# Third layer: the first unit of the second pass is prepared inside the first pass

## The chip, the cores and the metric

The kernel runs on one core of a Trainium2 chip. The metric is the device time of one execution in microseconds (us). Before the change three runs gave 3998.32, 4000.18 and 4005.41, so the median is 4000.18 us. One more execution was taken with the hardware profiler; every instruction time below is from it.

The engines go by these names: PE is TensorE, DVE is VectorE, ACT is ScalarE, POOL is GpSimd, SP is SyncE, which here only issues transfers (DMAs). Each engine works through its own queue in order and waits at the front of it. The queues run beside one another.

## The reference

The network has four layers over eight images of 56 x 56 positions and 192 channels. Each layer normalizes its input by groups of channels and adds its output to it. The change touches the third, a gated attention over windows of 8 x 8 positions:

```python
xw = _window_partition(x)
uvb = jax.nn.silu(xw @ W_uv + b_uv)
u, v, base = (uvb[..., :e], uvb[..., e:2 * e], uvb[..., 2 * e:])
qq = _rope2((base * gq_g + gq_b).reshape(-1, Wh, Ww, S), Wh, Ww).reshape(-1, N, S)
qk = _rope2((base * gk_g + gk_b).reshape(-1, Wh, Ww, S), Wh, Ww).reshape(-1, N, S)
lq = ...   # base * lq_g + lq_b, rotated by the position in the whole image
lk = ...   # the same with lk
attn = jnp.square(jax.nn.relu(jnp.einsum('bns,bms->bnm', qq * scale, qk) + rel_bias))
quadratic = attn @ v
lin_kv = jnp.einsum('bns,bne->bse', lk, v / (N * nW))
linear = lq @ jnp.sum(lin_kv, axis=0, keepdims=True)
out = u * (quadratic + linear) @ W_proj + b_proj
```

Here e is 384 and S is 128. A rotation (`_rope2`) is, in this kernel, `a * cos + b * sin`, where `a` and `b` are the base and the base with its halves exchanged, each after its own gain and offset. Since `lin_kv` is summed over all windows of all images, nothing of `linear` can be computed before every window has been seen once: that is why the layer has two passes.

## The kernel before

`layer2` handles the eight images as four pairs.

**First pass.** 52 turns (`groups`), each for up to 256 positions of both images of a pair. In turn n, TensorE projects the normalized input to values and base (`project`, L1560), into PSUM tiles of which there are three; a full turn takes two. VectorE adds the bias (`gates`, L1570) into a tile `sm`, of which there are two, and ScalarE applies Silu (L1571) into `vb`. The values are stored to device memory (`vst`, L1580). `keys` makes the rotated keys `l1`: two products and sums on GpSimd (L1589, L1590), two products on VectorE (L1594) and a sum there (L1597). Two turns later, in turn n + 2, `turn` transposes the base on TensorE (L1606) into a PSUM tile `t`, of which there is one, ScalarE copies it out (L1610) and SP stores it (`bst`, L1611); then `sum_up` adds keys times values to the running sum `kv` (L1620). The order inside a turn is written out by hand for all engines: the first projection, `turn`, `sum_up`, the jobs due in this turn, the other projections with their gates, the key tables, `keys`. `jobs` is a list of (turn, function) for work that is to be done beside the pass: weights, tables, bias rows, norms. The key tables (`key_tables`, L1530 to L1534) are prepared in turns 0, 1, 4, 7 and 10 and use a tile `tmp` of their own. Two further turns, 52 and 53, only transpose and sum. After them VectorE scales `kv` (L1669).

**Second pass.** 28 units, one for each strip of 448 positions of a pair. `fetch2` loads a unit's base (`bt`), the base with its halves exchanged (`bs`), its input `x` and its values `vt`; the loads of unit n + 2 are issued in unit n. For unit 0 the two base loads go through GpSimd's queue (L1688, L1690), all other loads through SP's. `prepare` makes three rotations: ScalarE makes `b` and `a` (L1704, L1705), GpSimd multiplies `b` by the sine table (L1715), VectorE multiplies `a` by the cosine table and adds (L1718, L1719). Then it normalizes the input (`normalize`, L1446). `attention` makes the window products (L1730), adds the bias (L1737) and squares (L1740). In unit n these are made for unit n + 1: ScalarE's part of the first two rotations stands in its queue ahead of unit n's first gate (`act`, L1793). The unit's own products (L1757, L1766, L1775, L1785) go to PSUM accumulators of which there are three, so that the second L1785 of a unit can start only when the first gate has been read out. Unit 0 has no unit before it: its loads, rotations, normalizing and attention stand between the passes. In the second pass TensorE, VectorE, ScalarE and GpSimd follow the written order, while the order of SP's transfers is left to the planner, which takes what is ready.

**Memory.** Pools of tiles are opened one after another and take memory in that order; in a pool the tiles lie in the order in which they are first asked for. When the first pass's pools are closed, the second pass's pools take the same bytes, and a tile waits for the users of whatever lay there. Before, the first pass opened `c1` (identity, key tables) ahead of `xp` (inputs), so the second pass's `bs` lay on the identity, which the last transposition reads.

## Time and profile before

| what | value |
|---|---|
| median of three runs | 4000.18 us |
| the profiled execution's own time | 4005.24 us |
| its span, first to last instruction | 4003.1 us |
| mean granted TensorE clock | 0.978 |
| first pass, first sum (L1620) to its last | 2578.4 to 2997.8 us from the start |
| second pass, first attention (L1730) to last output product (L1818) | 3012.3 to 3649.1 us |
| a full turn of the first pass | 8.57 us |
| a unit of the second pass | 22.17 us |

A row of a timeline reads: start, duration (both us), engine, line of the kernel, operation, written tile <- read tiles, partitions x elements, how many instructions were merged into the row, and in brackets how long the engine was idle before and what ended that. A row of a table of windows reads: the window, its length, the busy time of PE, PE's weight loads, DVE, ACT and POOL with the number of instructions, the granted clock as a share of full speed, the mean busy share of the 16 DMA engines and the GB/s that they moved. An engine's idle time costs nothing unless the engine that sets the end waits for it.

### The profile page before, as it was taken

To read this page: it belongs to the slowest core of one execution; us is meant where nothing else is said; L and a number is where in the kernel's file an instruction comes from. 1 tells how busy PE (TensorE), PEld (TensorE's weight loads), DVE (VectorE), ACT (ScalarE), POOL (GpSimd) and SP (SyncE) were. 2 spreads that over 40 slices of the span, in tenths; PEclk is the share of its full clock that TensorE was granted. 3 is DMA by queue.
4 is the path that set the end of the run, shared out by engine and by line. 5 is a ranking of instruction groups with operands and counts; after the bars stand their busy time and mean duration, and the time that the engine had idled before them with its cause. 6 is when DMAs were issued, how large, how long until landed. Compare 5 with 4: busy or idle time off the path is not lost. (4 is left out here: it accounts for less than half of the span.)

```text
span 4003.1 us, 115791 instructions
## 1 busy us (share of the span) xinstructions
PE 3763.2 (94%) x51036; PEld 2657.6 (66%) x51036; DVE 2400.7 (60%) x3270; ACT 1793.0 (45%) x2036; POOL 1517.7 (38%) x1325
## 2 busy tenths in 40 slices
PE   6989999999999999999799999899999999998997
PEld 4777767777776777777466666444444555556997
DVE  5646666565766666565544444576557777774664
ACT  2434444344444444443334433333335555553564
POOL 3222242222224232323433333333334545444776
PEclk9999999999999999999899999999999999999999
DMA  7856253333526343242433434556549767663333
GB/s 156 166 131 158 78 144 102 107 92 96 142 78 162 86 129 87 81 111 68 119 98 103 113 91 108 146 170 212 175 137 206 181 164 171 158 144 103 94 107 99
DMA packets 390300, 507.93 MB, mean 127 GB/s; under 512 B 176933, under 2 KB 326725, under 8 KB 388405
## 3 DMA queue, kind: packets, MB, share of 16 engines
q1 hardware_dynamic: 385621, 494.07, 48.1%
q8 instruction: 401, 6.57, 0.7%
q0 software_dynamic: 1040, 2.99, 0.3%
q10 hardware_dynamic: 3135, 3.47, 0.3%
q14 instruction: 103, 0.84, 0.1%
HBM read 344.69 MB, written 155.65 MB: 125 GB/s over the span
## 5 line engine op out<-in xcount | busy, mean ns | idle before, releaser
L384 POOL TENSOR_TENSOR qv<-s,s 128x392 f32<-128x392 f32 (+3 forms) x320 | 556.7, 1768 | 1282.1 <-ACT s L364 887.9
L356 PE MATMUL c<-x,wqv 64*128 64x392 f32 x2592 | 474.0, 511 | 12.3 <-ACT s L364 9.4
L356 PEld LDWEIGHTS c<-x,wqv 64*128 64x128 f32 x2592 | 254.2, 194 | 170.9 <-issue 13.5
L364 ACT ACTIVATE s<-c,bqv 128x784 f32<-128x784 f32 (+1 forms) x247 | 224.6, 912 | 246.8 <-PE c L356 188.0
L496 PE MATMUL c<-x,wp 64*128 64x224 f32 x2688 | 285.4, 358 | 24.5 <-DVE ot L474 13.3
L378 DVE TENSOR_TENSOR qv<-s,s 128x784 f32<-128x784 f32 (+1 forms) x160 | 242.2, 1529 | 98.4 <-ACT s L364 98.4
L416 DVE COPY ol<-c 56x1024 f32<-56x1024 f32 x184 | 221.1, 1210 | 104.2 <-PE c L411 104.2
L416 ACT COPY or<-c 56x1024 f32<-56x1024 f32 x184 | 183.6, 1007 | 220.4 <-DVE ol L416 219.4
L496 PEld LDWEIGHTS c<-x,wp 64*128 64x128 f32 x2688 | 256.9, 190 | 30.1 <-DVE ot L474 14.1
L520 DVE TENSOR_TENSOR s<-s,c 128x896 f32<-128x896 f32 x112 | 121.8, 1088 | 258.0 <-ACT s L503 237.2
L454 PEld LDWEIGHTS c<-or,ol 120*64 120x64 f32 x7168 | 217.3, 139 | 22.4 <-issue 16.0
L454 PE MATMUL c<-or,ol 120*64 120x56 f32 x7168 | 223.8, 224 | 7.3 <-DMA ol<-ed 4.1
L503 ACT ACTIVATE s<-c,bp 128x448 f32<-128x448 f32 x224 | 129.7, 630 | 205.9 <-PE c L496 203.3
L1571 ACT ACTIVATE vb<-sm 128x1024 f32<-128x1024 f32 (+1 forms) x100 | 103.9, 1040 | 263.3 <-issue 219.8
L2147 POOL TENSOR_TENSOR y<-y,s 128x448 f32<-128x448 f32 x168 | 185.0, 1101 | 87.2 <-ACT s L2126 87.2
L2116 PE MATMUL h<-ringv,am 128*64 128x57 f32 (+1 forms) x4400 | 191.0, 234 | 18.8 <-DVE ringv L2103 11.9
L1715 POOL TENSOR_TENSOR rs<-rs,sin_win 128x896 f32<-128x896 f32 x56 | 135.5, 2438 | 192.7 <-ACT rs L1704 192.7
L1560 PE MATMUL v<-wvb,wa 128*128 128x512 f32 (+1 forms) x400 | 194.4, 619 | 3.9 <-ACT wa L1446 3.5
L2116 PE MATMUL h<-ringh,am 128*64 128x57 f32 (+1 forms) x4400 | 185.5, 231 | 8.5 <-DVE ringh L2122 7.8
L1793 ACT ACTIVATE us<-c,bub 128x896 f32<-128x896 f32 x84 | 84.6, 1007 | 225.4 <-PE c L1775 142.1
L2116 PEld LDWEIGHTS h<-ringv,am 128*64 128x64 f32 x4400 | 166.6, 139 | 22.1 <-DVE ringv L2103 12.7
L1079 PE MATMUL c<-wv,xc 128*126 128x192 f32 x896 | 175.4, 339 | 0.0
(269 smaller groups left out, 7848.4 us busy)
## 6 DMA issues: line engine op xcount, KB each, us to landing
or<-tt SPq DMA_DIRECT2D x252, 196.0 KB
ol<-tt SPq DMA_DIRECT2D x252, 196.0 KB
vt<-v SPq DMA_DIRECT2D x56, 672.0 KB
v<-vb SPq DMA_DIRECT2D x96, 384.0 KB
x<-x SPq DMA_DIRECT2D x110, 168.0 KB
wqv<-in_l_w_qv SPq DMA_DIRECT2D x38, 384.0 KB
x<-in_x SPq DMA_DIRECT2D x64, 196.0 KB
x<-x SPq DMA_DIRECT2D x110, 112.0 KB
```

What stands on the lines that cost most here:

```text
L356: nc.tensor.matmul(ps[:, h, 0:n], wqv[q][rows, k, i, :], xn[rows, k, g * n : (g + 1) * n], start=(k == 0), stop=(k == 2),)
L364: nc.scalar.activation(t, ps[rows, :, 0:n], AF.Silu, bias=bqv[rows, j : j + 1])
L378: nc.vector.tensor_tensor(sub(qv[rows, 7 * g :, 64 + H - 1 :], (HH * 120, 2), (120, 7), (-1, H)), *(t.rearrange("p u (h w) -> p u h w", w= ...
L384: eng.tensor_tensor(sub(qv[rows, w0:, H - 1 - 7 * g - HH * u :], (120, w1 - w0), (-1, 7)), *(t[:, u].rearrange("p (h w) -> p w h", w=H)[:, ...
L416: copy(dst[:, :, :, i0 : i0 + 8], view[rows])
L454: nc.tensor.matmul(ps[u * 64 : (u + 1) * 64, k, v * H : (v + 1) * H], left[:, d * H : d * H + 64], right[:, d * H : (d + 1) * H], start=Tr ...
L496: nc.tensor.matmul(ps[:, h, u * n : (u + 1) * n], wps[j][rows, k, u, :], xn[rows, k, g * n : (g + 1) * n], start=(u == 0 and k == 0), stop ...
L1079: nc.tensor.matmul(out(i, u), group(i, u), wv[0], start=(u == 0), stop=True, skip_group_check=True,)
L1560: nc.tensor.matmul(out, x[:, at : at + n], wt, start=(k == 0), stop=(k == 1), skip_group_check=True,)
L1715: nc.gpsimd.tensor_tensor(view(b), view(b), tab[1], ALU.mult)
L2116: nc.tensor.matmul(ps[sides[c], y], am[a][:, m * CB : (m + 1) * CB], old[:, x], start=(n < 2), stop=True, skip_group_check=True,)
L2147: nc.gpsimd.tensor_tensor(v, v, line[:, j], ALU.add)
```

## The change

Unit 0's preparation becomes seven jobs of the first pass's last turns: in turn 46 its base is loaded (through SP), in turns 47, 48 and 49 one rotation each is made, in turn 50 its input is loaded, in turn 51 it is normalized, and in turn 52 the attention is made, in the PSUM tile `t`. The tiles for it are slots of the first pass's own pools where these are free, and a new pool `pre` for what must live on into the second pass (the third rotation, the attention, the normalized input). In the second pass these four kinds of tiles come in turns from `pre` (even units) and `wk` (odd units), one buffer in each instead of two in `wk`. `fetch2(0)` loads only the values, first, and the input, which the output needs. To make room, the key tables' `tmp` becomes a slot of `sm`, and `xp` is opened ahead of `c1`. `rotate` and `attention` now get their tiles from the caller, and the rotation's views have one dimension more.

```diff
+        pre = es.enter_context(tc.tile_pool(name="l2p", bufs=1, reuse_waits="tile"))
...
+        def rotate(r, bt, bs, i, a, b):
...
+            if i < 2:
+                view = lambda t: t.rearrange("p i (v t) -> p i v t", t=WT)
+                tab = [
+                    t.unsqueeze(1).unsqueeze(1).to_broadcast([S, 2, 7, WT]) for t in tables[0:2]
+                ]
...
+        def attention(qq, kk, pa, s, a):
...
+        def own(pool, shape, name):
+            return cx.tile(pool, shape, name, bufs=1)
...
+            xp = pool("l2x1", 2)
             c1 = pool("l2c1", 1)
-            xp = pool("l2x1", 2)
...
-                tmp = cx.tile(c1, [128, TW, S], "tmp")[:, 0:n]
+                tmp = cx.tile(wk, [128, 2, E + S], "sm").rearrange("p i e -> p (i e)")
+                tmp = tmp[:, 0 : n * S].rearrange("p (n s) -> p n s", s=S)
...
+            def lead_fetch():
+                t = cx.tile(xp, [CA, 2, 2 * SW], "xa")
+                bs, bt = lead["b"] = t[:, :, 0:SW], t[:, :, SW:]
+                cols = slice(0, SW)
+                for h in range(2):
+                    nc.sync.dma_start(bs[sides[h]], bst[0][sides[1 - h], :, cols])
+                nc.sync.dma_start(bt, bst[0][:, :, cols])
+
+            def lead_rotate(i):
+                if "r" not in lead:
+                    t = cx.tile(xp, [CA, 2, 2 * SW], "xa")
+                    lead["r"] = [t[:, :, 0:SW], t[:, :, SW:], own(pre, [S, 2, SW], "r2")]
+                bs, bt = lead["b"]
+                b = cx.tile(xp, [128, 2 * SW], "xb").rearrange("p (i t) -> p i t", i=2)
+                rotate(0, bt, bs, i, lead["r"][i], b)()
+
+            def lead_attend():
+                s = cx.tile(wk, [128, 512], "l2")[:, 0:SW].rearrange("p (v t) -> p v t", t=WT)
+                lead["at"] = own(pre, [128, 7, WT], "at")
+                attention(*lead["r"][0:2], cx.tile(psk, [128, 512], "t"), s, lead["at"])
+
+            def lead_load():
+                xa = cx.tile(xp, [CA, 2, 2 * SW], "wa")[:, :, 0:SW]
+                xb = cx.tile(xp, [128, 2 * SW], "wb")[:, 0:SW]
+                into(xa, xb, 0, 0, 1, nc.sync)
+                lead["x"] = xa, xb
+
+            last = len(groups)
+            jobs += [(last - 6, lead_fetch), (last - 2, lead_load), (last, lead_attend)]
+            jobs += [(last - 5 + k, lambda i=i: lead_rotate(i)) for k, i in enumerate((1, 0, 2))]
+            jobs += [
+                (last - 1, lambda: lead.update(xw=normalize(pre, 0, lead["x"], 1, bufs=1)))
+            ]
...
-            queue = nc.sync if n else nc.gpsimd
...
+            if n == 0:
+                vt = values()
+            else:
+                bs = cx.tile(xp, [S, 2, SW], "bs")
...
             x = load(xp, p, r, 1)
+            if n:
+                vt = values()
...
+        def side(n):
+            return wk if n % 2 else pre
...
-        todo = list(prepare(0))
-        do(todo)
-        ahead[0].append(attention(*ahead[0][2][0:2]))
+        x, _, _, vt = state.pop(0)
+        ahead[0] = [x, lead["xw"], lead["r"], vt, lead["at"]]
```

## The prediction

> **What bounds the kernel now.** I read the page's busy shares first, then the chain of work that ended last, then the timelines of single engines around the seam between the third layer's two passes, and last a table of windows over that seam.
>
> ```profile
> PE 3763.2 (94%) x51036; PEld 2657.6 (66%) x51036; DVE 2400.7 (60%) x3270; ACT 1793.0 (45%) x2036; POOL 1517.7 (38%) x1325
> ```
>
> TensorE is the bound, so only its pauses can be won. Its timeline shows one such pause at the seam:
>
> ```profile
> 2996.95 0.86 PE L1620 MATMUL kv<-vb,l 128*128 128x384 f32 x2
> 3012.30 1.76 PE L1730 MATMUL b<-r,r 128*64 128x64 f32 x28 [14.49 <-DVE r L1719]
> 3013.99 3.35 PE L1757 MATMUL c<-wa,wub 128*128 128x448 f32 x4
> 3017.14 2.20 PE L1766 MATMUL c<-r,kv 128*128 128x448 f32 x4
> 3021.64 0.99 PE L1785 MATMUL c<-at,vt 64*64 64x64 f32 x56
> 3024.17 1.67 PE L1766 MATMUL c<-r,kv 128*128 128x448 f32 x4
> ```
>
> The reader sees 14.49 us without a matmul, and then slow ones: L1757's four take 3.35 us where later ones take 1.67, the first attention 1.76 where the next (3030.50) takes 1.03. The windows say why, and what else is full:
>
> ```profile
> 2980.00:2997.00 17.00, 16.37 (x61) 7.87 (x59) 9.65 (x13) 5.97 (x8) 6.62 (x6) 1.00 0.38 130
> 2997.00:3003.00 6.00, 0.81 (x4) 0.20 (x2) 0.56 (x1) 0.70 (x2) 1.97 (x3) 0.85 0.95 267
> 3009.00:3015.00 6.00, 2.70 (x30) 2.18 (x31) 5.86 (x4) 4.21 (x6) 3.00 (x2) 0.50 1.08 233
> 3015.00:3021.00 6.00, 6.00 (x76) 3.06 (x78) 5.86 (x5) 4.91 (x5) 4.37 (x2) 0.73 1.10 234
> 3033.00:3045.00 12.00, 12.00 (x155) 6.34 (x152) 6.98 (x6) 6.71 (x7) 9.15 (x5) 1.00 0.49 97
> ```
>
> The last three columns are granted clock, DMA share and GB/s. The clock is 0.50 from about 3001 to 3018, and the DMA engines are full (0.95 to 1.10, 224 to 267 GB/s) until 3033: the seam is bound by transfers as much as by rotations. ScalarE shows who waits for them:
>
> ```profile
> 3014.91 1.13 ACT L1704 ACTIVATE rs<-bs,gbs 128x896 f32<-128x896 f32 x1 [0.71 <-DMA bs<-bs]
> 3016.30 1.13 ACT L1705 ACTIVATE r<-bt,gbs 128x896 f32<-128x896 f32 x1 [0.25 <-DMA bt<-bs]
> 3020.32 1.01 ACT L1793 ACTIVATE us<-c,bub 128x896 f32<-128x896 f32 x1 [0.84 <-PE c L1775]
> ```
>
> The first two rows already belong to unit 1; they stand in ScalarE's queue ahead of unit 0's first gate (third row), and unit 0's second product (L1785 at 3021.64) needs the accumulator that this gate frees.
>
> **What could be won at most.** An undisturbed unit without the output of a previous one takes 17.5 us (3038.50 to 3055.97 in the chain); unit 0 takes from 2997.81 to 3033.8, 36.0. With nothing late, 18.5 less 1.75 (the attention, below) = 16.8 us, 0.4%.
>
> **The rotations in turns 47 to 49.** VectorE's loop in a first-pass turn, with GpSimd's half:
>
> ```profile
> 2961.24 2.36 DVE L1570 TENSOR_TENSOR sm<-v,bvb 128x1024 f32<-128x1024 f32 x2 [1.41 <-PE v L1560]
> 2964.77 1.50 POOL L1589 TENSOR_TENSOR l<-vb,ta 128x512 f32<-128x512 f32 x1 [5.66 <-ACT vb L1571]
> 2966.35 1.33 POOL L1590 TENSOR_TENSOR l<-l,tn 128x512 f32<-128x512 f32 x1
> 2967.71 0.69 DVE L1597 TENSOR_TENSOR l<-l,l 128x512 f32<-128x512 f32 x1 [1.16 <-POOL l L1590]
> ```
>
> From gates to the end of L1597 the loop takes 7.16 us of a turn's 8.57; 1.41 is free. The change puts into it, in front of the next gates, GpSimd's product and VectorE's product and sum. These do not overlap:
>
> ```profile
> 3007.02 2.08 POOL L1715 TENSOR_TENSOR rs<-rs,sin_win 128x896 f32<-128x896 f32 x1 [1.18 <-ACT rs L1704]
> 3007.15 2.90 DVE L1719 TENSOR_TENSOR r<-r,rs 128x896 f32<-128x896 f32 x1
> 3009.97 1.08 DVE L1718 TENSOR_TENSOR r<-r,cos_win 128x896 f32<-128x896 f32 x1
> 3011.15 1.09 DVE L1719 TENSOR_TENSOR r<-r,rs 128x896 f32<-128x896 f32 x1
> ```
>
> A VectorE op beside a GpSimd one ends 0.95 after it (3009.10 to 3010.05). So the loop grows by 1.96 + 0.98 + 1.11 = 4.05 to 11.2, 2.65 over the period; after three turns the gates are 8.0 late. TensorE stands 4.41 behind the gates (2966.82, when it takes the PSUM buffer again, less 2962.41), so it loses 0.9 in turn 49 and 2.7 in turn 50. Turn 50 wins 1.4 back; turn 51 has only 5.2 us of TensorE work against a loop of 7.16, so the remaining 6.6 reach the last large sum (2994.16) whole. If the two engines overlapped, the loop would grow by 2.7 instead and about 1.6 would reach the sum. I take 6.6, because the 2.90 row is this very pair. ScalarE's two activations (1.12 each) lie in its idle 5.95 of a turn.
>
> The Trainium skill, "SBUF — State Buffer", section "Who interferes with whom", has a VectorE instruction with two SBUF inputs and a GpSimd one that reads SBUF exclude each other for a whole instruction, which speaks against this change and agrees with 2.90 against 1.09; overlap would lower the sum by 5.0.
>
> **The attention in turn 52.** 28 matmuls at 1.03, VectorE's add 0.62 and two hand-overs, because the last transpose needs the same PSUM buffer: 1.75 on the path, the square lies beside the last sum. The first pass thus ends at 2997.8 + 6.6 + 1.75 = 3006.2.
>
> **The restart.** Unit 0's values lie on the bytes of the rotated tiles, so their load (2 x 672 KB) can't be issued before the attention ends, about 3004.4. Before, the 19.0 us from 2997.3 to unit 1's last rotation input at 3016.3 carried about 4.4 MB, 232 GB/s. Now 0.92 MB (unit 0's bs and bt) is gone, and half a MB of x can go ahead; left after the last stores start at about 3002 are 0.5 MB of stores, 0.92 of unit 1's bs and bt, 1.34 of values, 0.23 of x: 3.0 MB at 240 GB/s (mean of the four rows from 2997 to 3021) is 12.5, plus 1 to land, an estimate: 3015.5, or 3017.4 with all x ahead of bt. I take 3016. Then three activations (3.2, from 3016.30 to 3019.48 before), the gate 1.05: L1785 runs at 3020.3 instead of 3021.64, 1.3 won. But TensorE has then been still from 3014.4 (stores, unit 1's bs and the values, 2.3 MB from 3002, landed at 3012.6, then 1.8 of work) and starts at half clock; the same 5.9 us at 0.50 (3012.3 to 3018.2) cost 2.9, so the seam ends 1.6 later than before. Bounds: bs and bt of unit 1 ahead of the values and no port loss: values at 3010, L1785's first run 10 earlier than its 3020.07, less 2.9: 7 won; the clock halved already in turns 50 to 52 (4.5 more, worked out below): 6.1 lost.
>
> **The table work at the start.** tmp now sits in a buffer of the gates' sums, so GpSimd's product, which ran ahead of its turn, waits for the first Silu of that turn.
>
> ```profile
> 2578.42 4.26 PE L1620 MATMUL kv<-vb,l 128*128 128x384 f32 x8 [7.22 <-DVE l L1597]
> 2575.84 1.98 POOL L1531 TENSOR_TENSOR tmp<-tb,gk 128x768 f32<-128x768 f32 x1
> ```
>
> Turn 1: this product moves to about 2579.4; L1597 before it gets shorter (2.10 to 0.69, 1.4 won), then six ops of 0.94 to 1.96 follow one another and L1597(1) ends 2.7 later, so the second sum (2588.50) starts 1.2 late. Turn 4: 2.5 later, inside the slack. Turn 7: 4.0 later, 2648.2 against a sum at 2647.05: 1.2. Turns 0 (waits for a DMA at 2567.40 anyway) and 10 (128 elements): nothing. Together 2.4; between 1.4 won and 5.
>
> **At nothing.** SP: three loads in turn 46 (1.9 us of issue) and six in turn 50 (3.0) stand ahead of stores that wait for ScalarE until 2956.15 and 2990.41, with SP idle from 2950.5 and 2983.3; uncovered, 3.0. Their 1.6 MB meet a DMA share of 0.30 to 0.44. Normalizing: 2.15 in an idle 3.92 of ScalarE in turn 51. GpSimd's three issues (1.98) go. The reshaped view: products with 14x64 and 2x448 tables took 2.06 and 2.08. Alternating pools: two buffers as before. Units 1 to 27: 22.17 us of TensorE without a pause, so what the seam gives or takes stays.
>
> **Sum.** 2.4 + 1.6 = 4.0 us slower. The profiled execution took 4005.24 (span 4003.1, 2.1 around it), 5.1 above the median of 4000.18 and inside the runs' 3998.32 to 4005.41; I add to the median: 4004.2.
>
> **The rivals.**
> - *The restart is clean (faster).* Unit 1's bs and bt get ahead of the values and the port costs little: for it, SP is not ordered by hand in the second pass, and 1.41 us a turn is free; against it, the 2.90 row. 7 won plus 1.4 at the start is 3991.8; with the clock kept up as well, up to 14 won, 3986.
> - *The clock falls inside the first pass (slower).* The pauses of 2.7 halve it from turn 50 on: the sum of 2.58, the attention, and the last transposition and sum double, 2.58 + 1.03 + 0.9 = 4.5 more, 4008.7; with 5 at the start 4011.3. For it: at 2608 to 2612 a pause of 1.66 beside small matmuls was followed by 0.51 (2612 to 2614). It decides from 4 us of such loss.
>
> **How the numbers follow.** 0.2% is 8.0 us, about what a measurement of this kernel tells from no change. My forecast, that the pause only moves, gets 0.58 and alone would span 3993 to 4008 (7 won and 1.4 at the start gone, to the point where the slower rival decides); the faster rival gets 0.17 and the slower 0.25, since a pause of 2.7 is longer than the one that was followed by 0.51. The range 3990 to 4011 takes in both rivals' prices and leaves out about 0.1 at each end: a clean restart with the clock kept up, and a halved clock with the full price at the start.
>
> **What would show it.** Right: rotation products of 2 to 3 us on VectorE in turns 47 to 49, gates late by about 2.7 more each turn, the last sum near 3006, a pause before unit 0's second L1785 with ScalarE waiting for bs or bt, clock 0.5 after it. Wrong: first-pass turns that stay at 8.57, or ScalarE's gate not held up by unit 1's loads.

## The result and the profile after

The changed kernel takes 4015.75 us (median of five runs, 4013.92 to 4023.99) where the kernel before takes 4000.18 on the same chip (five runs, 3998.32 to 4005.41). The ratio is 1.0036, interval 1.0024 to 1.0047: 14 us slower, outside the predicted 3990 to 4011. The profiled execution took 4015.75 us, its span is 4014.0.

TensorE's work is as before, from the page of the changed kernel:

```profile
PE 3769.7 (94%) x51036; PEld 2660.8 (66%) x51036; DVE 2398.4 (60%) x3270; ACT 1792.6 (45%) x2036; POOL 1516.7 (38%) x1322
```

To see where the time comes from, the third layer is cut at eight events of the two traces, and the stretches are laid side by side. All lengths are in us; a start is meant where nothing else is said. The sums are those of TensorE for turn n of the first pass (L1670 after, L1620 before), the gates are VectorE's (L1620 after, L1570 before), a unit's output product is L1854 (L1806 before), the next layer's first matmul L2176 (L2116).

| stretch | before | after | difference | predicted |
|---|---|---|---|---|
| A: end of the last matmul of the layer before, to the sum of turn 7 | 96.6 | 96.6 | 0.0 | +2.4 |
| sum of turn 7 to the gates of turn 46 | 305.6 | 305.7 | +0.1 | 0 |
| B: gates of turn 46 to gates of turn 51 | 41.3 | 47.6 | +6.2 | +6.6 |
| C: gates of turn 51 to the end of the last sum | 3.8 | 7.4 | +3.6 | +1.75 |
| D: end of the last sum to unit 0's output product | 33.6 | 31.7 | -1.9 | -6.75 |
| E: unit 0's to unit 27's output product | 610.6 | 611.9 | +1.4 | 0 |
| F: unit 27's output product to the next layer's first matmul | 17.7 | 21.8 | +4.1 | 0 |
| sum | 1109.2 | 1122.7 | +13.5 | +4.0 |

What follows F differs by 0.2 us. What comes ahead of A, where nothing was changed, was 2.5 us shorter in the trace after (2548.0 against 2550.4), so that the spans differ by 10.9 and not by 13.5; this part is 2542.7 to 2554.2 long in the traces of this document. The loss lies in B and C, as predicted but for 0.4 us less and 1.85 more, in D, where 4.9 us less was won than predicted, and in E and F, where nothing had been predicted. A, where 2.4 had been predicted, shows nothing. The letters are used below.

**B.** VectorE's timeline of the changed kernel around turn 47, and GpSimd's:

```profile
2956.80 2.55 DVE L1647 TENSOR_TENSOR l<-l,l 128x512 f32<-128x512 f32 x1 [1.17 <-POOL l L1640]
2959.27 1.08 DVE L1510 TENSOR_TENSOR xa<-xa,cos_win 128x896 f32<-128x896 f32 x1
2960.45 1.09 DVE L1511 TENSOR_TENSOR xa<-xa,xb 128x896 f32<-128x896 f32 x1
2961.47 2.35 DVE L1620 TENSOR_TENSOR sm<-v,bvb 128x1024 f32<-128x1024 f32 x2
2972.61 2.35 DVE L1620 TENSOR_TENSOR sm<-v,bvb 128x1024 f32<-128x1024 f32 x2
```

```profile
2956.72 2.08 POOL L1507 TENSOR_TENSOR xb<-xb,sin_win 128x896 f32<-128x896 f32 x1
```

The gates come 11.14 us apart (2961.47, 2972.61) instead of 8.57, where the prediction had a loop of 11.2. But it is not the rotation that meets GpSimd's product: the product starts 0.08 us ahead of the key sum L1647 of the turn before, and that sum takes 2.55 instead of 0.69. The rotation's own two operations take 1.08 and 1.09.

**C and D.** TensorE's timeline of the changed kernel at the seam, and ScalarE's:

```profile
2998.03 4.54 PE L1670 MATMUL kv<-vb,l 128*128 128x384 f32 x8 [2.59 <-DVE l L1647]
3002.50 1.04 PE L1521 MATMUL t<-xa 128*64 128x64 f32 x28
3004.27 0.33 PE L1656 MATMUL t<-ident,vb 128*128 128x128 f32 x1 [0.73 <-DVE l L1526]
3013.42 1.66 PE L1833 MATMUL c<-at,vt 64*64 64x64 f32 x51 [3.15 <-DMA vt<-v]
3025.34 1.77 PE L1833 MATMUL c<-at,vt 64*64 64x64 f32 x56 [8.66 <-ACT us L1841]
3027.04 2.86 PE L1805 MATMUL c<-wa,wub 128*128 128x448 f32 x4
```

```profile
3018.28 1.13 ACT L1494 ACTIVATE rs<-bs,gbs 128x896 f32<-128x896 f32 x1 [13.34 <-DMA bs<-bs]
3021.21 1.13 ACT L1495 ACTIVATE r<-bt,gbs 128x896 f32<-128x896 f32 x1 [1.79 <-DMA bt<-bs]
3024.30 0.98 ACT L1841 ACTIVATE us<-c,bub 128x896 f32<-128x896 f32 x1
```

The last large sum waits 2.59 us and takes 4.54 instead of 2.85: half clock. The attention (L1521) and the last transposition, which waits for its PSUM buffer, take the predicted 1.75. Then TensorE stands 8.66 us before unit 0's second product, because unit 0's first gate (L1841) stands in ScalarE's queue behind unit 1's inputs, and unit 1's bt lands at 3021.2. The table of windows shows clock, DMA share and GB/s in its last columns:

```profile
2994.00:3002.50 8.50, 5.91 (x16) 2.63 (x12) 4.04 (x7) 3.80 (x7) 3.78 (x4) 0.80 0.56 184
3005.00:3015.00 10.00, 6.06 (x77) 3.31 (x79) 0.56 (x1) 0.00 (x0) 0.00 (x0) 0.86 1.06 217
3015.00:3025.00 10.00, 1.68 (x14) 0.21 (x7) 2.52 (x2) 4.92 (x5) 3.62 (x2) 0.50 1.08 238
```

**F.** ScalarE at the start of the next layer, first before, then after; u is that layer's input tile `u0`:

```profile
3650.06 2.99 ACT L2065 ACTIVATE u<-y,co 128x3136 f32<-128x3136 f32 x1
```

```profile
3664.58 3.01 ACT L2125 ACTIVATE u<-y,co 128x3136 f32<-128x3136 f32 x1 [7.49 <-DMA x<-xb]
```

Before, ScalarE goes from unit 27's last activation straight to u. After, it and the two other engines that write u wait until unit 27's last store of x has landed.

### The profile page after: what moved, and what is told of

Its sections match the earlier page's. It is cut to its first block, busy times and chain, and to the rows that moved or that the text cites. A ratio compares the mean times of both kernels' runs of the same rounds, so it can differ in the third digit from the quotient of the medians.

```text
span 4014.0 us, 115799 instructions
## 1 busy us (share of the span) xinstructions
PE 3769.7 (94%) x51036; PEld 2660.8 (66%) x51036; DVE 2398.4 (60%) x3270; ACT 1792.6 (45%) x2036; POOL 1516.7 (38%) x1322
## 4 chain that ended last, share of the span: by engine, by line
PE 79%; DVE 8%; issue 3%; ACT 3%; DMA 3%; SPq 2%; POOL 2%; ACTq 0%; POOLq 0%; DVEq 0%
PE c L356 10%; PE h L2176 6%; PE v L1610 6%; PE c L496 5%; PE c L454 4%; PE o L529 4%; PE c L1079 4%; PE o L356 3%; PE c L1805 3%; PE y L1114 3%; PE c L1866 3%; PE c L1814 3%; PE kv L1670 2%; PE c L550 2%; PE c L1085 2%
## 5 line engine op out<-in xcount | busy, mean ns | idle before, releaser
L454 PEld LDWEIGHTS c<-or,ol 120*64 120x64 f32 x7168 | 217.3, 139 | 22.9 <-issue 17.7
L2176 PE MATMUL h<-ringv,am 128*64 128x57 f32 (+1 forms) x4400 | 191.0, 234 | 22.2 <-DVE ringv L2163 15.3
L2176 PE MATMUL h<-ringh,am 128*64 128x57 f32 (+1 forms) x4400 | 185.3, 231 | 8.7 <-DVE ringh L2182 7.8
L1841 ACT ACTIVATE us<-c,bub 128x896 f32<-128x896 f32 x84 | 84.6, 1007 | 226.1 <-PE c L1823 141.2
L2176 PEld LDWEIGHTS h<-ringv,am 128*64 128x64 f32 x4400 | 166.5, 139 | 25.5 <-DVE ringv L2163 16.2
```

The lines of the kernel that those rows point to most:

```text
L454: nc.tensor.matmul(ps[u * 64 : (u + 1) * 64, k, v * H : (v + 1) * H], left[:, d * H : d * H + 64], right[:, d * H : (d + 1) * H], start=Tr ...
L2176: nc.tensor.matmul(ps[sides[c], y], am[a][:, m * CB : (m + 1) * CB], old[:, x], start=(n < 2), stop=True, skip_group_check=True,)
```

## The experiments

All runs in one table: the ratio to the kernel before with its 95% interval, and the stretches A to F of the profiled execution. "Changed" means that an edit stands on the changed kernel, "before" that it stands on the kernel before.

| run | on | ratio | A | B | C | D | E | F |
|---|---|---|---|---|---|---|---|---|
| kernel before | | 1 | 96.6 | 41.3 | 3.8 | 33.6 | 610.6 | 17.7 |
| changed kernel | | 1.0036 (1.0024 to 1.0047) | 96.6 | 47.6 | 7.4 | 31.7 | 611.9 | 21.8 |
| e1_tmp | changed | 1.0021 (1.0008 to 1.0034) | 93.7 | 47.6 | 7.4 | 31.6 | 612.3 | 21.8 |
| e9_before_swap | before | 0.9992 (0.9982 to 1.0002) | 92.3 | 41.3 | 3.8 | 34.3 | 610.6 | 17.7 |
| e2_rest | changed | 1.0016 (1.0004 to 1.0027) | 96.6 | 43.6 | 7.3 | 31.8 | 614.3 | 21.9 |
| e10_ab | changed | 1.0017 (1.0006 to 1.0028) | 96.8 | 43.6 | 7.3 | 32.4 | 611.0 | 21.9 |
| e12_hold | changed | 1.0008 (0.9998 to 1.0018) | 96.6 | 41.4 | 5.7 | 32.2 | 611.9 | 21.8 |
| e3_order | changed | 1.0018 (1.0008 to 1.0028) | 97.0 | 47.6 | 7.4 | 26.2 | 612.1 | 21.8 |
| e8_act | changed | 1.0024 (1.0010 to 1.0039) | 96.3 | 47.6 | 5.7 | 28.2 | 613.3 | 21.8 |
| e4_layout | changed | 1.0022 (1.0011 to 1.0033) | 96.9 | 47.6 | 7.4 | 31.5 | 610.5 | 17.7 |
| e5_before_vt | before | 1.0013 (1.0002 to 1.0024) | 96.7 | 41.3 | 3.8 | 34.2 | 610.7 | 21.8 |
| e6_all | changed | 0.9984 (0.9975 to 0.9992) | 91.5 | 43.6 | 7.3 | 27.0 | 610.6 | 17.7 |
| e7_pool | changed | 0.9981 (0.9972 to 0.9991) | 94.4 | 43.6 | 5.7 | 27.1 | 612.0 | 17.8 |
| e11_best | changed | 1.0006 (0.9994 to 1.0017) | 94.1 | 43.6 | 7.4 | 29.5 | 610.9 | 17.8 |
| e13_late | changed | 1.0021 (1.0007 to 1.0034) | 93.0 | 41.4 | 5.7 | 26.0 | 627.8 | 17.8 |
| e14_hold_all | changed | 0.9974 (0.9961 to 0.9986) | 93.6 | 41.4 | 5.7 | 25.5 | 612.3 | 17.8 |
| e15_values | changed | 0.9976 (0.9965 to 0.9987) | 92.7 | 41.4 | 5.7 | 25.8 | 611.5 | 17.8 |

A ratio of 0.001 is 4 us, so the intervals alone seldom tell one edit from another; the verdicts below rest on the stretches, each of one profiled execution, which hold still where nothing was edited: B and F to 0.1, A to 0.4 (but 91.5 to 94.4 with e1's edit, of which below), D to 0.9, C to the one step of 1.7 that is told of at the end. E is not read: its intervals from unit to unit are the same 22.2, 23.7 and 24.9 us in these kernels but for the one from unit 11 to 12 (22.2 to 26.0, and unlike in kernels that do the same there; in the changed kernel TensorE waits 1.24 us in it for VectorE), and the first ones in e8 (23.5) and e13.

### The start of the first pass: e1_tmp and e9_before_swap

```diff
-                tmp = cx.tile(wk, [128, 2, E + S], "sm").rearrange("p i e -> p (i e)")
+                tmp = own(pre, [S, 2, SW], "r2").rearrange("p i e -> p (i e)")
```

> Edit: the table work's tmp no longer takes a slot of the gates' sums but the idle bytes of unit 0's third rotation (r2), so it has one buffer of its own as before. Theory (traces): the table work costs nothing, since the seventh sum ends 478.3 us after turn 1's last projection both before (2647.05 less 2568.79) and after (2644.59 less 2566.25). Then this kernel takes what the changed one took, 4015.75 within 2 us. Rival (the prediction's step): 2.4 us at the pass's start are real and were masked by something else that got faster; then the seventh sum comes about 2 us sooner after turn 1 and the time is about 4013.3.

A falls by 2.9 and the ratio to 1.0021: the rival is right (the theory's 478.3 should read 78.3). The tmp in `sm` does cost time, and something else in the change wins as much. e9 puts the order of the two pools alone into the kernel before:

```diff
+            xp = pool("l2x1", 2)
             c1 = pool("l2c1", 1)
-            xp = pool("l2x1", 2)
```

> Edit: the kernel before, with the first pass's x pool laid ahead of its constants' pool, as the changed kernel has it, and nothing else. Theory: the constants (gk and the tables) then lie on bytes that the layer before gives up earlier; this alone lets the table work start some 4 us sooner after that layer's last matmul, and the seventh sum comes 2.5 to 3 us sooner (93.7 to 94.1 instead of 96.6 after it), which is what hid the cost of tmp. Time: 2 to 3 less than before. Rival: the earlier first sum comes with the fewer loads on GpSimd's or SP's queue of the changed pass; then 96.6 as before and the time of before.

A falls by 4.4, more than expected; the time (0.8 in 1000 faster) just misses being told from no change. ScalarE in the kernel before, and then in e9:

```profile
2558.05 1.41 ACT L1446 ACTIVATE wb<-xb,norm 128x448 f32<-128x448 f32 x2 [3.51 <-DMA x<-x]
2560.15 0.34 ACTq L1627 DMA_DIRECT2D gk<-in_l_lk_gb  x1
```

```profile
2552.02 1.41 ACT L1446 ACTIVATE wa<-xa,norm 128x448 f32<-128x448 f32 x2 [7.90 <-DMA x<-x]
2555.14 0.34 ACTq L1627 DMA_DIRECT2D gk<-in_l_lk_gb  x1
```

The load of gk, the gains of the keys, is issued from ScalarE's queue behind the normalizing. Before, the last tile of that normalizing waited a second time (3.51) for a store of the layer before out of its bytes, and gk landed only at 2567.40, when GpSimd's first product of the tables could begin. With `xp` first, that second wait is gone.

Not all of 2.9 and 4.4 belongs to the edits. Between the sums of turns 3 and 4 TensorE does the small matmuls of a normalization, behind a pause. These are the windows from the one sum to the other in the kernel before, the changed kernel, e1, e9 and e6 (which does the same there as e1); the granted clock is the third figure from the end:

```profile
2605.64:2619.34 13.70, 12.04 (x45) 6.01 (x43) 11.88 (x15) 4.25 (x5) 4.57 (x3) 0.88 0.46 156
2601.18:2616.31 15.13, 13.70 (x45) 7.21 (x43) 14.67 (x15) 3.82 (x5) 8.11 (x4) 0.77 0.50 164
2594.84:2608.66 13.82, 12.04 (x44) 6.00 (x43) 12.02 (x15) 4.25 (x5) 4.70 (x3) 0.88 0.47 157
2605.14:2615.89 10.75, 10.40 (x45) 5.51 (x43) 10.49 (x14) 3.65 (x4) 3.67 (x2) 1.00 0.48 167
2596.07:2608.21 12.14, 10.40 (x44) 5.52 (x43) 11.89 (x15) 3.65 (x4) 4.67 (x3) 1.00 0.54 179
```

TensorE's busy time (10.40, 12.04 or 13.70) counts spells of 3.4 us at half clock: one in the kernel before, two in the changed kernel, one in e1, none in e9 and e6. Each costs 1.65 us, and e1 and e6 show that the same kernel code gets one or none. One such spell less is in e1's 2.9 and in e9's 4.4, so that 1.3 and 2.7 are left without it. Over all traces, A is 96.3 to 97.0 in the seven changed kernels without e1's edit (mean 96.7) and 91.5 to 94.4 in the seven with it (93.3); for the order of the pools there is the one trace.

### The last turns of the first pass: e2_rest, e10_ab and e12_hold

e2 issues VectorE's part of a rotation behind the gates of its turn:

```diff
-                rotate(0, bt, bs, i, lead["r"][i], b)()
+                lead["rest"] = rotate(0, bt, bs, i, lead["r"][i], b)
...
                         gates(g + s, pvs[s], vb, s)
+                    if "rest" in lead:
+                        lead.pop("rest")()
```

> Edit: in turns 47 to 49 VectorE's product and sum of a rotation are issued behind the turn's gates, not ahead of them; nothing else moves. Theory: the first pass ends late because the gates stand behind GpSimd's product and VectorE's two operations. Then the last sum ends 44 to 46 us after turn 47's gates (52.2 in the changed kernel, 42.6 before), the time falls by 6 to 8 to 4008 to 4010, and the large sum that took 4.54 takes 2.6 again because TensorE no longer pauses before it. Rival: GpSimd's product holds VectorE up wherever it lies (it now runs beside the gates and the key products), the turns stay above 10.5 us and the time stays within 2 us of 4015.75.

Between the two: B falls by 4.0, not by 6 to 8, the turns take 9.0 and 9.8, and the large sum still takes 4.53 after the same pause of 2.59. VectorE's key sum still meets GpSimd's product (timeline of VectorE, e2):

```profile
2959.52 2.55 DVE L1647 TENSOR_TENSOR l<-l,l 128x512 f32<-128x512 f32 x1 [1.16 <-POOL l L1640]
2969.45 2.38 DVE L1647 TENSOR_TENSOR l<-l,l 128x512 f32<-128x512 f32 x1
```

e10 adds to e2 the other order of ScalarE's two activations (`a` first), so that the product's input comes later:

```diff
-            nc.scalar.activation(b, bs, AF.Identity, bias=g[3], scale=g[1])
+            if b_first:
+                nc.scalar.activation(b, bs, AF.Identity, bias=g[3], scale=g[1])
             nc.scalar.activation(a, bt, AF.Identity, bias=g[2], scale=g[0])
+            if not b_first:
+                nc.scalar.activation(b, bs, AF.Identity, bias=g[3], scale=g[1])
...
+                lead["rest"] = rotate(0, bt, bs, i, lead["r"][i], b, False)
```

> Edit: the changed kernel with VectorE's part of a rotation behind the gates (as in the run on that), and ScalarE making a rotation's two inputs in the other order, so that the one that GpSimd multiplies comes 1.1 us later. Theory: with the product no longer ready beside VectorE's last key sum, it runs beside the gates, which read PSUM, and costs VectorE nothing: that key sum takes 0.69 instead of 2.4 in turns 46 to 48, the turns stay at 8.6, the gates of turn 51 come 41.3 to 42 us after those of turn 46 (43.6 with VectorE's part behind the gates alone, 47.6 in the changed kernel), the pause before the last large sum shrinks from 2.59 to below 1 and that sum runs at full clock. Rival: GpSimd's product holds VectorE up beside the gates just as well; then 43.6 stays.

B stays at 43.6, as the rival said, but not for its reason, as the timelines of GpSimd and VectorE in e10 show: the input still came in time, and the product got ahead by 0.07 us.

```profile
2957.37 2.07 POOL L1510 TENSOR_TENSOR xb<-xb,sin_win 128x896 f32<-128x896 f32 x1
2957.44 2.55 DVE L1650 TENSOR_TENSOR l<-l,l 128x512 f32<-128x512 f32 x1 [1.16 <-POOL l L1643]
```

So the run did not put the question. e12 does: e2 with a copy that makes GpSimd wait for the key sum.

```diff
+                held = own(pre, [128, 7, WT], "at")
+                nc.gpsimd.tensor_copy(held[:, 0], kept[max(kept)][1][:, 0, 0, 0:WT])
```

> Edit: VectorE's part of a rotation behind the gates (as before), and a small GpSimd copy ahead of GpSimd's product that reads the last key sum of VectorE, so that the product can't start before that sum has ended and runs beside the gates. (Making the two inputs in the other order had left the product ready at 2957.4, still ahead of the key sum at 2957.44.) Theory: what is left of the lateness is only the product that gets ahead of VectorE's key sum (2.4 to 2.55 instead of 0.69); now that sum takes 0.69, and the gates of turn 51 come 41.3 to 42 us after those of turn 46 (43.6 without the copy). Rival: a product beside the gates blocks VectorE all the same, the time only moves: 43 or more.

B is 41.4, that of the kernel before. GpSimd and VectorE in e12:

```profile
2973.32 0.24 POOL L1706 COPY at<-l 128x64 f32<-128x64 f32 x1 [1.14 <-DVE l L1647]
2973.58 2.09 POOL L1507 TENSOR_TENSOR xb<-xb,sin_win 128x896 f32<-128x896 f32 x1
2972.56 0.69 DVE L1647 TENSOR_TENSOR l<-l,l 128x512 f32<-128x512 f32 x1
2973.66 2.36 DVE L1620 TENSOR_TENSOR sm<-v,bvb 128x1024 f32<-128x1024 f32 x2 [0.40 <-PE v L1610]
```

The product runs beside the gates and neither is longer for it (2.09 and 2.36). The whole of B was thus two things: VectorE's 2.2 us ahead of the gates, and a product that blocked the key sum. The Trainium skill, "SBUF — State Buffer", section "Who interferes with whom", states both halves: two SBUF inputs on VectorE contend with a GpSimd operation that reads SBUF, and at most one SBUF input, outside VectorE's 2-port modes, does not. The gates have one, and 2.36 beside the product against 2.36 alone agrees; the prediction used only the first half. C falls to 5.7: the pause is 0.65, the large sum takes 2.85, and 1.9 is left, about the attention's 1.75. The ratio of 1.0008 can't be told from no change.

### The restart: e3_order, e8_act and what came of them

e3 issues unit 1's bs and bt ahead of everything of unit 0; the tiles stay where they were:

```diff
             if n == 0:
+                vt = cx.tile(xp, [128, 7, E], "vt")
+                x = cx.tile(xp, [CA, 2, SW], "xa"), cx.tile(xp, [128, SW], "xb")
+                lead["next"] = bases(0, slice(SW, 2 * SW))
+                values(vt)
+                into(*x, p, r, 1, nc.sync)
```

> Edit: SP issues unit 1's bs and bt ahead of unit 0's values and x; the tiles keep their bytes. Theory: the restart is late because of SP's order, in which bt stands behind the values and six loads of x. Then ScalarE's wait of 13.3 us for bs and TensorE's of 8.7 us for the gate are gone, unit 0's output matmul starts 24 to 27 us after the last sum (34.2 in the changed kernel, 35.9 before), and the time falls by 7 to 10, to 4006 to 4009. Rival: the transfers' total rate sets it, so the values land later by what now goes ahead of them (0.92 MB at 240 GB/s, 3.8 us), and at most 3 us are won: 4013 or more.

D is 26.2, 5.5 less, and the ratio is lower by 7 us. (The expectation counts to the output matmul L1866, which starts 34.0 us after the last sum in the changed kernel; here it is 28.6.) So the waits for bs and for the gate go as the theory had it, but its 24 to 27 us is missed by 1.6, and the rival's 3 us at most is passed. ScalarE's gate now runs at 3011.75, ahead of TensorE's need, but the values come later than they did (TensorE, e3; the last sum ends at 3003.7):

```profile
3013.18 0.47 PE L1839 MATMUL c<-at,vt 64*64 64x64 f32 x2 [5.55 <-DMA vt<-v]
3016.41 1.66 PE L1839 MATMUL c<-at,vt 64*64 64x64 f32 x51 [2.76 <-DMA vt<-v]
```

TensorE waits 8.3 us for the values where it waited 3.9, so 4.4 are given back, about the rival's 3.8: both the order and the rate count. e8 changes ScalarE's order instead:

```diff
-            rests = [next(todo, None) for _ in range(2)]
+            rests = [next(todo, None) for _ in range(2)] if n else []
...
             g0.act()
+            if n == 0:
+                rests = [next(todo, None) for _ in range(2)]
```

> Edit: the changed kernel with one thing changed: ScalarE runs unit 0's first gate ahead of unit 1's first rotation inputs; SP's order stays. Theory: TensorE's pause of 8.7 us before unit 0's second product is only ScalarE's queue (the gate behind activations that wait for bs and bt), so the pause goes, unit 0's products run at full clock, and its output matmul starts 22 to 25 us after the last sum (31.7). Rival: bs and bt are needed for unit 1's attention soon after, so that the pause only moves behind unit 0's products and the output matmul starts no earlier than 29 us after the last sum.

Nearly the rival: D is 28.2, and the interval to the next unit's output product grows by 1.3 (23.5 instead of 22.2). The pause of 8.66 is gone and comes back as one of 4.00 a few products later, in which the second gate stands behind the same inputs (TensorE and ScalarE, e8):

```profile
3025.78 3.35 PE L1805 MATMUL c<-wa,wub 128*128 128x448 f32 x4 [4.00 <-ACT us L1841]
3018.34 1.13 ACT L1494 ACTIVATE rs<-bs,gbs 128x896 f32<-128x896 f32 x1 [8.23 <-DMA bs<-bs]
```

Four kernels then tried to get below 26 with other queues. All have tmp on r2's bytes, VectorE's part behind the gates, and the tile order of e4 below; each diff shows a part of what is its own. e7: values, then bs and bt on GpSimd's queue, and e8's order on ScalarE.

```diff
+            queue = nc.sync if n else nc.gpsimd
...
-                    nc.sync.dma_start(vt[sides[i]], src)
+                    queue.dma_start(vt[sides[i]], src)
...
+                    queue.dma_start(bs[sides[h]], bst[p][sides[1 - h], :, cols])
...
+                queue.dma_start(bt, bst[p][:, :, cols])
```

> Edit: as the one with the four edits, but unit 0's values and unit 1's bs and bt (in this order) are issued by GpSimd's queue, where they don't stand behind SP's last store of bs, and ScalarE runs unit 0's first gate ahead of unit 1's rotation inputs. Theory: at the seam only the order of two queues (SP's and ScalarE's) is lost time, so unit 0's output matmul starts 18 to 21 us after the last sum (31.7 in the changed kernel, 26.2 with unit 1's bs and bt first), the clock stays at 1.0 and the time is 4 to 8 less than with the four edits. Rival: with both queues free the transfers (2.3 MB at some 240 GB/s) hold the values or bs back: 24 us or more after the last sum.

D is 27.1, the rival's: the values are issued as early as 2997.9 and land at 3007 and 3010, beside SP's x.

e11: the same with unit 0's x and unit 1's fetch on GpSimd's queue too, and e10's order. The diff's minus line is e7's.

```diff
-            queue = nc.sync if n else nc.gpsimd
+            queue = nc.sync if n > 1 else nc.gpsimd
...
+                into(*x, p, r, 1, queue)
```

> Edit: all that helped so far in the changed kernel: tmp on r2's bytes, VectorE's part behind the gates with the two inputs in the other order, x buffers ahead of the values, ScalarE's first gate ahead of unit 1's inputs, and units 0 and 1 fetched by GpSimd's queue in the order values, bs, bt, x, x, values. Theory: the seam's transfers (values 1.34 MB, then 0.92 MB) then get the DMA engines ahead of x, so unit 0's output matmul starts 21 to 24 us after the last sum (27 in the two kernels that combine), and with 2 to 4 us less in the first pass the ratio to before is 0.996 to 0.997. Rival: the transfers at the seam share the engines with x and stores in whatever order they are issued: 26 us or more, ratio 0.998.

Worse, 29.5: values and bt land earlier (3004.4 and 3007.8), but unit 1's products now stand in GpSimd's queue behind twelve loads of x and two of values, until 3014.6.

e13: GpSimd's queue with those products ahead of the x, unit 2's loads and unit 3's bs and bt on it as well, and e12's copy.

```diff
+            if n == 0:
+                do(lead["late"], 1)
             do(rests, 1)
...
             rests.append(next(todo, None))
+            if n == 0:
+                do(lead["late"])
+                state[2] = fetch2(2)
```

> Edit: all that helped (tmp on r2's bytes, VectorE's part behind the gates with the copy, x buffers ahead of the values, ScalarE's first gate ahead of unit 1's inputs), and GpSimd's queue issues unit 0's values and unit 1's bs and bt first, unit 1's two products next, and only then the x of units 0 and 1, unit 1's values and unit 2's tiles, which SP had issued at once. Theory: what the seam waits for is 2.3 MB behind other transfers; with nothing else asked for, the values land within 7 us and bt within 11 of their issue, unit 0's output matmul starts 20 to 23 us after the last sum (27.1 at best so far), and the ratio to before is 0.995 to 0.997. Rival: values, bs and bt alone fill the engines for the time that is lost, so it stays at 26 or more and the ratio at 0.998.

D is 26.0, the rival's, and the loads that were put off cost the next two units 15.5 us (33.8 and 26.1 instead of 22.2 each), so that the ratio is 1.0021.

e15: values on GpSimd's queue, bs and bt at once on SP's, e8's order, e12's copy.

```diff
+            queue = nc.sync if n else nc.gpsimd
...
-                    nc.sync.dma_start(vt[sides[i]], src)
+                    queue.dma_start(vt[sides[i]], src)
```

> Edit: as the one before, but GpSimd's queue issues unit 0's values (beside SP, which issues unit 1's bs and bt ahead of x), and ScalarE runs unit 0's first gate ahead of unit 1's inputs. Theory: values and bs, bt then start together within 3 us and share the engines only with the last stores, so that unit 0's output matmul starts 23 to 26 us after the last sum and the ratio is 0.996 to 0.997. Rival: the 2.3 MB and the rotations of unit 1 behind them fill the time in any order: 26 to 28 us, a ratio as in the kernel above.

D is 25.8, just inside the theory's range, but no less than with SP's queue alone (25.5 in e14 below), and the ratio is e14's, as the rival had it. From 2993.0 to 3004.3, when the second half of the values is there, its DMA engines are full:

```profile
2993.00:3004.30 11.30, 5.61 (x39) 2.53 (x33) 1.81 (x3) 1.27 (x2) 0.56 (x1) 0.97 0.99 214
```

So once the order is mended, D stays near 26, with TensorE still waiting 5.0 us (e15) to 8.3 us (e14) for the values: some 6 us below the changed kernel and 8 below the kernel before, and no order that was tried gets further. Values that are there before the first pass ends were not tried; their tile takes 10.5 KB in each partition.

### The start of the next layer: e4_layout and e5_before_vt

e4 asks for the x tiles ahead of the values, and issues the transfers in the changed kernel's order:

```diff
             if n == 0:
+                x = cx.tile(xp, [CA, 2, SW], "xa"), cx.tile(xp, [128, SW], "xb")
                 vt = values()
...
+                into(*x, p, r, 1, nc.sync)
```

> Edit: the second pass asks for its x buffers ahead of its values, so that the next layer's u0 lies over values, bs and bt and no longer over x; and unit 0's values no longer lie over the rotated tiles. Theory: the next layer starts 4.2 us later after the change because u0 has to wait for the last unit's stores of x out of its bytes. Then from the last output matmul of this layer to the next layer's first matmul of that line the time is back from 15.1 to about 10.9; and the values can be fetched before the attention, so that bt lands some 5 us earlier: 4015.75 less 4.2 less 3 to 5, 4006 to 4009. Rival: the later start of the next layer follows from the later end of this one (the queue of stores), not from the bytes: 15 us stay there and the time is above 4010.

(The expectation counts F from the last L1866, 6.7 us later than the table.) F is 17.7 again, exactly that of before, in a layer that ends as late as in the changed kernel. The second half of the theory failed: D is 31.5, because bs and bt stayed behind all of unit 0's x. e5 puts the fault into the kernel before:

```diff
+            vt = cx.tile(xp, [128, 7, E], "vt")
             bs = cx.tile(xp, [S, 2, SW], "bs")
...
             x = load(xp, p, r, 1)
-            vt = cx.tile(xp, [128, 7, E], "vt")
```

> Edit: the kernel before, with nothing changed but that the second pass asks for its values' buffers first, so that the last unit's x lies on bytes that the next layer's u0 takes. Theory: these bytes alone cost the next layer's start 4 us, whatever the seam does: from the last output matmul to the next layer's first matmul 21.8 us as in the changed kernel instead of 17.7, and the time about 4 us over that of before. Rival: the late start came with the changed seam; then 17.7 us and the time of before within 2 us.

F is 21.8 and the ratio 1.0013 (1.0002 to 1.0024), 5 us, with nothing else moved by more than 0.6 (D). ScalarE and TensorE in e5, then ScalarE in e4:

```profile
3651.69 3.01 ACT L2065 ACTIVATE u<-y,co 128x3136 f32<-128x3136 f32 x1 [7.44 <-DMA x<-xb]
3657.84 1.49 PE L2116 MATMUL h<-ringv,am 128*64 128x114 f32 x20 [14.64 <-DVE ringv L2103]
```

```profile
3651.74 2.99 ACT L2126 ACTIVATE u<-y,co 128x3136 f32<-128x3136 f32 x1
```

So F is the bytes and nothing else. In the kernels' memory plans u0 takes bytes 114816 to 153804 of each partition. Before, values and rotations lay there (in e4 values, bs, bt and rotations); in the changed kernel and in e5, with the values asked for first, the last x tiles lie there, among them the one of unit 27 that is stored last.

### Together: e6_all and e14_hold_all

e6 has the edits of e1, e2, e3 and e4.

> Edit: the four edits so far together in the changed kernel (tmp on r2's idle bytes; VectorE's part of a rotation behind the gates; unit 1's bs and bt ahead of unit 0's values and x; x buffers asked for ahead of the values). Theory: they touch four different places, so their gains add up: 2.9 at the pass's start, 4.0 in turns 47 to 51, 5.5 and the wait for values (some 5) at the seam, 4.1 and 1.4 behind it: 18 to 23 us less than the changed kernel, so 3993 to 3998 where that took 4015.75, a ratio to before of 0.998 to 1.000. Rival: they share a limit (transfers at the seam, the lock between VectorE and GpSimd), so that half of it comes: 4004 to 4007.

From A to F it is 19.4 us shorter than the changed kernel, within the theory's 18 to 23, and faster than the kernel before: 0.9984 (0.9975 to 0.9992), where 0.998 to 1.000 was expected. The sum is right in part by luck: D gave 4.7 where 5.5 and some 5 more were expected, and A gave 5.2 for 2.9, because two half-clock spells fell away between the sums of turns 3 and 4. e14 adds e12's copy.

> Edit: the kernel with the four edits (tmp on r2's bytes; VectorE's part behind the gates; unit 1's bs and bt ahead of unit 0's values and x; x buffers ahead of the values), plus the GpSimd copy that holds the product back. Theory: the copy wins the same 2.3 us of gates and, with the last large sum at full clock, 1.7 more; nothing else moves: some 4 us less than with the four edits, a ratio to before of 0.997 to 0.998. Rival: the seam takes it back, since its transfers don't start sooner: ratio 0.998 to 0.999 and 30 us from the last sum to unit 0's output matmul instead of 27.

0.9974 (0.9961 to 0.9986), 10 us faster than before and with e15 (0.9976) the best of all: B and C win 3.9 where 4.0 was expected, and D does not take it back (25.5). What is left of the seam is TensorE's wait for the values:

```profile
2989.04 2.85 PE L1670 MATMUL kv<-vb,l 128*128 128x384 f32 x8 [0.64 <-DVE l L1647]
3004.06 0.47 PE L1843 MATMUL c<-at,vt 64*64 64x64 f32 x2 [5.58 <-DMA vt<-v]
3007.28 1.66 PE L1843 MATMUL c<-at,vt 64*64 64x64 f32 x51 [2.75 <-DMA vt<-v]
```

## Why the prediction was wrong, and where it was right

The sign of the forecast and its picture of the seam were right (the pause moves, the first pass pays for it), the size was not: +4.0 against +13.5 in the traces. Three steps failed: the restart, which was to win 6.75 and won 1.9; "Units 1 to 27 ... so what the seam gives or takes stays", where 4.1 were lost behind the last unit; and the clock in the first pass, which the sum had at 0 and which cost 1.7. A fourth error went the other way: the swap of the pools was costed at nothing and won back what the table work cost. Step by step:

- **The table work at the start, +2.4: partly right as a price, wrong as a sum.** Undoing it wins 2.9 in one trace and 3.4 as a mean of seven; turns 1 and 7, priced at 1.2 each, gave 1.0 and 0.6 in e1, and most of the rest is the clock. The step that failed is "Turns 0 (waits for a DMA at 2567.40 anyway)": that DMA is gk, and the change itself moved its issue, by opening `xp` first, from 9.7 to 2.7 us after the last matmul of the layer before. The prediction read the wait as fixed and costed the swap of the pools at nothing. Alone it wins 4.4 in A, or 2.7 without a half-clock spell that e9 lacks.
- **The rotations, +6.6: right in size.** 6.2 in B, with a loop of 11.14. The row it rested on (2.90, two engines excluding each other) named the right cause; what is blocked is the key sum, not the rotation, whose operations take 1.08 and 1.09, so that the first sign that was to show it right, rotation products of 2 to 3 us, was not seen.
- **The attention, +1.75: right.** 1.9 of C is left in e12.
- **The clock inside the first pass.** This was the slower rival, at up to 4.5. About 1.7 of it came, in the one sum behind the pause of 2.59. The forecast itself had 0 for it.
- **The restart, -6.75: the largest error within a step; -1.9 came.** The mis-sized term is the 12.5 us for 3.0 MB from 3002, with bt there at 3016, 9.8 us after the last sum; it was there 16.0 us after it. The values were issued at 3003.6, 1.7 us ahead of the last sum's end as in the prediction. But SP issued none of the x ahead of them; it issued all of x behind them and bs and bt behind that (bt at 3014.05), and the next x was already sharing the engines when bt was on its way. From 3003.6 to bt's landing at 3021.2, 17.6 us at 214 GB/s moved 3.8 MB: at the prediction's 240 GB/s the bytes it had left out are 3.2 us and the lower rate 1.9. From there on the chain is as predicted: three activations, the gate, a second product at half clock, 2.86 for four matmuls that take 1.67 otherwise.
- **"Units 1 to 27 ... what the seam gives or takes stays": wrong by 4.1.** The step looked at work and not at bytes. Another layout of the same tiles changed what the next layer's first tile waits for.
- **E, +1.4.** It is one interval, in which TensorE waits for VectorE, and it comes and goes between kernels that do the same there. Nothing ties it to the change.

The faster rival had about the right price for a mended order and port: it gave 8 to 14 us, and e14 is 10 us faster than before, of which A has 3.1 and B to D have 6.2 in the traces. But the change as made mended neither.

## What to carry to other kernels

When a change opens pools or asks for tiles in another order, compare for each large tile what lay on its bytes before and after, and at both ends of the stage: here one change of order (the pools) won 2.7 to 4.4 us at one end and another (values ahead of x) lost 4.1 at the other, and the waits that moved are at lines that were not edited. Work put into an engine's loop beside another stage goes behind what the bound engine waits for, and here a GpSimd operation on SBUF belonged beside the VectorE operations that read PSUM. When loads are moved to a busy seam, write down the order in which one queue will issue them and add up the bytes up to the one that is needed, those of the next unit too.

## What the runs showed of the hardware

- A GpSimd product that starts 0.07 or 0.08 us ahead of a VectorE sum with two SBUF inputs makes it 2.55 us long instead of 0.69; beside the gates, which have one SBUF input, neither took longer (2.09 and 2.36, e12).
- The granted clock falls in whole spells: 3.4, 6.8, 10.2 and 17.1 us at 0.50 are the lengths around the seam in these traces, and within an execution all starts and ends of spells lie whole multiples of 3.413 us apart. The same pause of 2.6 us ahead of the same sum was followed by half clock in the changed kernel and seven others (C of 7.3 or 7.4, 4.4 or 4.5 us for the sum), and by full clock in e7 and e8 (2.85 us). On that grid of 3.413 us, 2.2 to 2.6 us of the pause lie within one window in the eight, while it is split into 0.7 and 1.9 in e7 and into 1.6 and 1.0 in e8. The Trainium skill, "TensorE: Matmul & The Clock Gate", section "What's actually happening", has free-running windows of 3413 ns, which agrees: in these ten traces, where the pause falls on the grid tells whether it costs 1.7 us or nothing.
